# Feature-major copies of a graph network's inputs: TensorE transposes exchanged for VectorE blocks and trips through DRAM

## The chip, the cores and the metric

One core of one Trainium2 chip. The metric is the device time of one execution in microseconds; each kernel was run several times and the median is quoted. A ratio is the mean time of one kernel's fast runs over that of the other's of the same rounds, so it is not quite the ratio of the medians quoted beside it.

## The reference

64 graphs of 256 nodes with 128 features pass through four layers that share one adjacency matrix; each layer ends in `layernorm(x + layer(x))`.

```python
def reference(x, adj, ...):                        # x (64, 256, 128), all float32
    x = layernorm(x + pair_attention(x, adj, ...))          # layer 0
    x = layernorm(x + graph_attention(x, adj, ...))         # layer 1
    x = layernorm(x + gated(x, adj, ...))                   # layer 2, five steps of:
    #   m = adj @ h; u = h @ U3; z = sigmoid(m @ W3 + u); r = sigmoid(m @ W4 + u)
    #   h = (1 - z) * h + z * tanh(m @ W5 + (r * h) @ U5)
    x = layernorm(x + chebyshev(x, adj, ...))               # layer 3: x, adj@x, adj@adj@x, ...
    return x
```

The kernel's products over features read x with features on the partitions ("feature-major"); its products with the adjacency read it with nodes there ("token-major"). Turning one into the other is what the change is about.

## The kernel before

A unit is two graphs, a tile of 128 by 512 floats. There are 32 units and seven lanes, so seven units are in flight. The order of instructions on every engine is fixed at build time by a small list scheduler, the planner, with booked durations and latencies. TensorE transposes each layer's input:

```python
    def feature_major(u, L, name="xT0"):            # layers 0, 2 and 3 call it
        ps = bank()
        for g in range(G):                           # G = 4
            add(PE, 110, lambda g=g: nc.tensor.transpose(
                ps.ap[:, g * P : (g + 1) * P], X[u].ap[:, g // NC, g % NC, :], ident.ap), (X[u], ident), (ps,))
        add(ACT, 500, lambda: nc.scalar.copy(L[name].ap, ps.ap), (ps,), (L[name],))
        return L[name]
```

Inside the gated layer the way back to token-major already went through DRAM for most units: VectorE turns 32 by 32 blocks (705 ns for a tile in the profile of this kernel), one store puts them in a DRAM tile, four loads collect them in another order. I call this a trip.

```python
            if step < STEPS - 1 and u < NU - NEAR:   # NEAR = 3, NU = 32
                add(DVE, 600, lambda h=h, v=v: nc.vector.transpose(...), (h,), (v,))
                add("sp", 450, lambda v=v: nc.sync.dma_start(L["hb"].ap, v.ap), (v,), (L["hb"],))
                for a in range(D // BL):             # four loads
                    add("sp", 450, lambda a=a: nc.sync.dma_start(...), (L["hb"],), (ht,), wait=1000)
                continue
```

How the planner books this:

```python
    LATENCY = {"pe": 700, "dve": 600, "act": 600, "pool": 700, "sp": 5000}
    OWN = {"pe": 0, "dve": 70, "act": 70, "pool": 100, "sp": 0}
    # end of a task = start + its ns + LATENCY of its engine + its wait
    def seen_at(self, t, by):                        # when `by` may start after `t`
        return t.end if t.eng != by.eng else t.off + self.OWN[t.eng]
```

All transfers are issued by one engine, "sp" (SyncE's queue).

The softmax here doesn't subtract the row's maximum and nothing guards it: scores larger than these inputs give would overflow.

## Time and profile before

| | before |
|---|---|
| median | 1518.3 us |
| span of the profiled run | 1511.7 us |
| TensorE busy / rest of the span | 1470.5 / 41.2 us |
| TensorE's waits for trips | 11.2 us in 10 waits |
| granted TensorE clock | 0.997 |

TensorE is the bound: busy 97% of the span.

### The profile page before, as it was taken

What the parts mean: (1) busy time and instruction counts of PE and PEld (TensorE: products, weight loads), DVE (VectorE), ACT (ScalarE), POOL (GpSimd) and SP (SyncE); (2) the same over time, 40 slices, a digit from 0 to 9 for tenths busy, and PEclk for the clock granted to TensorE, in tenths of its full rate; (3) what the DMA queues carried; (4) which work ended last, traced back from release to release, by engine and by line L of the source; (5) the groups of instructions that cost most, each with busy time, mean ns of one, the idle gap of its engine ahead of it and who ended that gap; (6) DMA issues with size and microseconds to landing.
All of it is one profiled execution on the core that took longest, in us unless ns stands there. A gap on an engine that the chain in (4) does not pass through costs nothing.

```text
span 1511.7 us, 18346 instructions
## 1 busy us (share of the span) xinstructions
PE 1470.5 (97%) x6081; PEld 993.9 (66%) x6081; DVE 1028.4 (68%) x2485; ACT 762.8 (50%) x1455; POOL 148.8 (10%) x134
## 2 busy tenths in 40 slices
PE   8899998999999999999999999999999999999998
PEld 7565575666567576666666675766666666665566
DVE  6975648876666776767667777677577767664554
ACT  4664435655545554456454555456355554554432
POOL 0200011110001011010010110101001001000011
PEclk9999999999999999999999999999999999999999
DMA  5123323223232323232332233232332322220001
GB/s 151 27 67 76 77 49 73 57 61 79 56 87 55 75 65 84 50 81 70 74 73 60 65 71 85 47 76 66 71 67 53 75 59 62 58 56 15 15 8 42
DMA packets 323952, 95.93 MB, mean 63 GB/s; under 512 B 267409, under 2 KB 301457, under 8 KB 323857
## 3 DMA queue, kind: packets, MB, share of 16 engines
q1 hardware_dynamic: 323856, 94.76, 27.6%
q8 instruction: 48, 0.79, 0.2%
q14 instruction: 48, 0.39, 0.1%
HBM read 55.67 MB, written 39.03 MB: 63 GB/s over the span
## 4 chain that ended last, share of the span: by engine, by line
PE 87%; DMA 5%; DVE 4%; SPq 2%; ACT 1%; issue 0%; POOLq 0%; DVEq 0%
PE ps L635 42%; PE ps L615 20%; PE ps L703 7%; PE ps L710 4%; PE ps L547 3%; PE ps L577 3%; PE ps L413 2%; PE ps L481 2%; PE ps L591 2%; PE ps L542 1%; DMA ht<-hb 1%; SPq L670 1%; DMA hb<-p 1%; PE ps L677 1%; DVE st L446 0%
## 5 line engine op out<-in xcount | busy, mean ns | idle before, releaser
L635 PE MATMUL ps<-m,gT 128*128 128x512 f32 x960 | 464.3, 593 | 1.3 <-ACT m L631 0.9
L451 POOL TENSOR_TENSOR rstd<-ve,nhalf 128x4 f32<-128x4 f32 x128 | 148.1, 1159 | 1357.6 <-DVE ve L448 1303.8
L635 PEld LDWEIGHTS ps<-m,gT 128*128 128x128 f32 x960 | 175.7, 190 | 139.7 <-issue 119.3
L615 PE MATMUL ps<-adjTp,ht 128*128 128x256 f32 x928 | 234.2, 380 | 11.8 <-DMA ht<-hb 11.2
L615 PEld LDWEIGHTS ps<-adjTp,ht 128*128 128x128 f32 x928 | 172.4, 190 | 90.9 <-issue 64.4
L654 DVE TENSOR_TENSOR p<-p,xT 128x512 f32<-128x512 f32 x160 | 109.8, 687 | 130.8 <-ACT p L648 130.5
L650 ACT ACTIVATE e<-ps,bias 128x512 f32<-128x512 f32 x160 | 109.8, 686 | 131.6 <-PE ps L635 131.2
L641 ACT ACTIVATE e<-ps,bias 128x512 f32<-128x512 f32 x160 | 109.7, 686 | 125.5 <-PE ps L635 125.2
L631 ACT COPY m<-ps 128x512 f32<-128x512 f32 x160 | 93.5, 584 | 151.8 <-PE ps L615 151.6
L635 PE MATMUL ps<-xT,gT 128*128 128x512 f32 x320 | 162.2, 593 | 2.4 <-ACT xT L415 1.3
L635 PE MATMUL ps<-e,u5T 128*128 128x512 f32 x320 | 162.5, 593 | 1.6 <-DVE e L643 1.6
L643 DVE SCALAR_TENSOR_TENSOR e<-e,xT 128x512 f32<-128x512 f32 x160 | 109.2, 684 | 77.7 <-ACT e L641 77.7
L648 ACT ACTIVATE p<-ps,bias 128x512 f32<-128x512 f32 x160 | 109.9, 687 | 82.0 <-PE ps L635 76.8
L615 PE MATMUL ps<-adjT,x 128*128 128x256 f32 x512 | 142.1, 380 | 0.0
L655 DVE SCALAR_TENSOR_TENSOR p<-e,p 128x512 f32<-128x512 f32 x160 | 109.3, 684 | 21.0 <-ACT e L650 18.6
L657 DVE SCALAR_TENSOR_TENSOR xT<-p,xT 128x512 f32<-128x512 f32 x160 | 109.6, 686 | 2.4
L615 PEld LDWEIGHTS ps<-adjT,x 128*128 128x128 f32 x512 | 84.3, 191 | 38.5 <-issue 25.7
L446 DVE BATCH_NORM_STATS2 st<-ps 128x6 f32<-128x256 f32 x128 | 53.3, 425 | 70.1 <-PE ps L710 51.2
L415 ACT COPY xT<-ps 128x512 f32<-128x512 f32 x96 | 55.9, 584 | 72.4 <-PE ps L413 72.0
L635 PEld LDWEIGHTS ps<-e,u5T 128*128 128x128 f32 x320 | 58.7, 190 | 48.2 <-issue 35.2
L566 ACT ACTIVATE e<-m,esd 128x256 f32<-128x256 f32 x116 | 84.3, 760 | 8.1 <-DMA m<-row 8.1
L413 PE MATMUL ps<-ident,x 128*128 128x128 f32 x384 | 82.4, 277 | 2.6 <-DMA x<-in_x_dram 2.5
(131 smaller groups left out, 1954.5 us busy)
## 6 DMA issues: line engine op xcount, KB each, us to landing
hb<-p SPq DMA_DIRECT2D x116, 256.0 KB, 2.1
ht<-hb SPq DMA_DIRECT2D x464, 64.0 KB, 2.5
m<-row SPq DMA_DIRECT2D x58, 256.0 KB, 3.6
x<-in_x_dram SPq DMA_DIRECT2D x32, 256.0 KB, 3.3
out_dram<-x SPq DMA_DIRECT2D x32, 256.0 KB, 2.4
u<-rowu SPq DMA_DIRECT2D x58, 3.8 KB, 3.1
row<-cu SPq DMA_DIRECT2D x29, 2.0 KB, 2.1
rowu<-cu SPq DMA_DIRECT2D x29, 4.0 KB, 1.7
```

Source lines behind the costliest of these rows:

```text
L413: add(PE, 110, lambda g=g: nc.tensor.transpose(ps.ap[:, g * P : (g + 1) * P], X[u].ap[:, g // NC, g % NC, :], ident.ap), (X[u], ident), (ps,))
L451: add(POOL, 1050, lambda: nc.gpsimd.tensor_tensor(rstd.ap, ve.ap, nhalf.ap, op=ALU.pow), (ve, nhalf), (rstd,))
L615: add(PE, mm_ns(N), lambda b=b, mc=mc: nc.tensor.matmul(ps.ap[:, b * N : (b + 1) * N], lhs(b, mc), mat.ap[:, mc, :], start=(mc == 0), stop ...
L635: add(PE, mm_ns(T), lambda: nc.tensor.matmul(ps.ap, w(), rhs.ap, start=start, stop=stop, skip_group_check=True), (c, rhs), (ps,))
L641: add(ACT, 600, lambda ps_g=ps_g: nc.scalar.activation(r.ap, ps_g.ap, AF.Tanh, bias=bias2.ap[:, 1:2], scale=0.5), (ps_g, bias2), (r,))
L643: add(DVE, 600, lambda h=h: nc.vector.scalar_tensor_tensor(r.ap, r.ap, 1.0, h.ap, op0=ALU.add, op1=ALU.mult), (r, h), (r,))
L648: add(ACT, 600, lambda ps_v=ps_v: nc.scalar.activation(v.ap, ps_v.ap, AF.Tanh, bias=bias2.ap[:, 2:3]), (ps_v, bias2), (v,))
L650: add(ACT, 600, lambda ps_g=ps_g: nc.scalar.activation(z.ap, ps_g.ap, AF.Tanh, bias=bias2.ap[:, 0:1], scale=0.5), (ps_g, bias2), (z,))
L654: add(DVE, 600, lambda h=h: nc.vector.tensor_sub(v.ap, v.ap, h.ap), (v, h), (v,))
L655: add(DVE, 600, lambda: nc.vector.scalar_tensor_tensor(v.ap, z.ap, 1.0, v.ap, op0=ALU.add, op1=ALU.mult), (v, z), (v,))
L657: add(DVE, 600, lambda h=h, new=new: nc.vector.scalar_tensor_tensor(new.ap, v.ap, 0.5, h.ap, op0=ALU.mult, op1=ALU.add), (v, h), (new,))
L703: add(PE, mm_ns(N), lambda k=k, src=src, c=c, b=b: nc.tensor.matmul(view(c)[:, :, b, :], bn(src.ap)[:, b, c * P : (c + 1) * P], w3.ap[:, k ...
```

## The change

The intent is to take transposes off the bounding engine. Layer 0's x is loaded in four blocks of 32 features, so that one VectorE transpose of 32 by 32 blocks finishes it (701 ns in the profile after; the first seven units still use TensorE). The inputs of layers 2 and 3 of units 3 to 30 are turned by VectorE and a trip. The border of the gated layer's own trips moves to the same units. Also, the load of the x that a lane needs next moves from before layer 0 to after it, and x gets separate tiles (`zs`) to land in.

```diff
-NEAR = 3
+NEAR = 1
 ...
     def load_x(u):
+        z = zs[u % LANES]
+        if u < LANES:
+            add("sp", 1000, lambda: nc.sync.dma_start(z.ap..., x_u[u]), (), (z,))
+            return
+        for a in range(D // BL):
+            add("sp", 450, lambda a=a: nc.sync.dma_start(z.ap[a * BL : (a + 1) * BL]..., x_a[u, a]...), (), (z,), wait=1000)
 ...
+    def far(u):
+        return DIRECT <= u < NU - NEAR               # DIRECT = 3
+    def turned(u, L, name="xT0"):                     # layers 2 and 3
+        t = L[name]
+        if not far(u):
+            feature_major(X[u], ..., t)
+            return t
+        v = L["v"]
+        add(DVE, 1050, lambda: nc.vector.transpose(
+            v.ap.rearrange("p (a g i) -> p g a i", g=G, i=BL),
+            X[u].ap.rearrange("p b c (j a) -> p (b c) a j", j=BL)), (X[u],), (v,))
+        add("sp", 450, lambda: nc.sync.dma_start(L["hb"].ap, v.ap), (v,), (L["hb"],))
+        for q in range(P // BL):
+            add("sp", 450, lambda q=q: nc.sync.dma_start(t.ap...[:, :, q], L["hb"].ap[...]...), (L["hb"],), (t,), wait=1000)
+        return t
 ...
     def layer0(u, L):
-        xT = feature_major(u, L)
+        xT, z = L["xT0"], zs[u % LANES]
+        if u < LANES:
+            feature_major(z, ..., xT)
+        else:
+            add(DVE, 600, lambda: nc.vector.transpose(xT.ap, z.ap), (z,), (xT,))
 ...
-            if step < STEPS - 1 and u < NU - NEAR:
+            if step < STEPS - 1 and far(u):
```

More of the change, by code (lines that the diff above doesn't have):

```diff
@@ L223 @@
     x_u = x.rearrange("(u b) (c p) d -> u p b c d", b=UB, p=P)
+    x_a = x.rearrange("(u b) n (a i) -> u a (b n) i", b=UB, i=BL)
     out_u = out.rearrange("(u b) (c p) d -> u p b c d", b=UB, p=P)
-    xs, X = [cell(f"x{k}", [P, UB, NC, D]) for k in range(2 * LANES)], {}
+    zs = [cell(f"z{k}", [P, T]) for k in range(LANES)]
     def load_x(u):
-        X[u] = c = xs[u % len(xs)]
-        add("sp", 1000, lambda: nc.sync.dma_start(c.ap, x_u[u]), (), (c,))
+        z = zs[u % LANES]
+        if u < LANES:
+            add("sp", 1000, lambda: nc.sync.dma_start(z.ap.rearrange("p (b c d) -> p b c d", b=UB, c=NC), x_u[u]), (), (z,))
+            return
+        for a in range(D // BL):
+            add("sp", 450, lambda a=a: nc.sync.dma_start(
+                z.ap[a * BL : (a + 1) * BL].rearrange("j (b i) -> j b i", i=BL),
+                x_a[u, a].rearrange("(b j) i -> j b i", j=BL)), (), (z,), wait=1000)
     w1 = load("w1", W, [D, D])
@@ L387, in lane_cells @@
             c[name] = Cell(c[at].ap.rearrange("p g n -> p (g n)")[:, half * T : (half + 1) * T])
+        c["x"] = cell(f"x_{k}", [P, UB, NC, D])
         c["h0"] = cell(f"h0_{k}", [P, G, C0])
@@ L399, in lane_cells @@
         return c
+    X = {}
     lanes = [lane_cells(k) for k in range(LANES)]
@@ L407, in bn, with feature_major @@
         return ap.rearrange("p (b n) -> p b n", b=UB)
-    def feature_major(u, L, name="xT0"):
+    def far(u):
+        return DIRECT <= u < NU - NEAR
+    def feature_major(src, view, t):
         ps = bank()
         for g in range(G):
-            add(PE, 110, lambda g=g: nc.tensor.transpose(
-                ps.ap[:, g * P : (g + 1) * P], X[u].ap[:, g // NC, g % NC, :], ident.ap), (X[u], ident), (ps,))
-        add(ACT, 500, lambda: nc.scalar.copy(L[name].ap, ps.ap), (ps,), (L[name],))
-        return L[name]
+            add(PE, 110, lambda g=g: nc.tensor.transpose(ps.ap[:, g * P : (g + 1) * P], view(g), ident.ap),
+                (src, ident), (ps,))
+        add(ACT, 500, lambda: nc.scalar.copy(t.ap, ps.ap), (ps,), (t,))
+    def turned(u, L, name="xT0"):
+        t = L[name]
+        if not far(u):
+            feature_major(X[u], lambda g: X[u].ap[:, g // NC, g % NC, :], t)
+            return t
[5 more added lines that the diff above has]
+        for q in range(P // BL):
+            add("sp", 450, lambda q=q: nc.sync.dma_start(
+                t.ap.rearrange("p (g q i) -> p g q i", g=G, i=BL)[:, :, q],
+                L["hb"].ap[q * BL : (q + 1) * BL].rearrange("j (a g i) -> (j a) g i", g=G, i=BL)),
+                (L["hb"],), (t,), wait=1000)
+        return t
     def to_row(row, src, view, n):
@@ L469, in layer0 @@
     def layer0(u, L):
-        xT = feature_major(u, L)
+        xT, z = L["xT0"], zs[u % LANES]
+        if u < LANES:
+            feature_major(z, lambda g: gd(z.ap)[:, g], xT)
+        else:
+            add(DVE, 600, lambda: nc.vector.transpose(xT.ap, z.ap), (z,), (xT,))
+        X[u] = L["x"]
         xb = bn(xT.ap)
@@ L619, in layer2 @@
     def layer2(u, L):
-        h, ht = feature_major(u, L), X[u]
+        h, ht = turned(u, L), X[u]
         for step in range(STEPS):
@@ L625, in layer2 @@
                     left(ps_m, ht, b)
-                elif u < NU - NEAR:
+                elif far(u):
                     left(ps_m, ht, b, lambda b, mc: gd(ht.ap)[:, b * NC + mc], adjTp)
@@ L687, in layer3 @@
     def layer3(u, L):
-        xT = feature_major(u, L)
+        xT = turned(u, L)
         ps_a, aT, s = bank(), L["m"], L["z"]
@@ L716, in spawn @@
     def spawn(u, lane):
-        if u + LANES < NU:
-            load_x(u + LANES)
         for k, layer in enumerate((layer0, layer1, layer2, layer3)):
@@ L721, in spawn @@
             layer(u, lanes[lane])
+            if not k and u + LANES < NU:
+                load_x(u + LANES)
     def first(t):
```

## The prediction

> **What bounds the kernel now.** I read the page's busy shares first, then TensorE's waits, then a stretch of TensorE's timeline to get the price of one transpose, then the queue of DMA issues, because the change takes work from TensorE and gives it to that queue. Busy shares (engine, busy us, share of the span, instructions):
>
> ```profile
> span 1511.7 us, 18346 instructions
> ...
> PE 1470.5 (97%) x6081; PEld 993.9 (66%) x6081; DVE 1028.4 (68%) x2485; ACT 762.8 (50%) x1455; POOL 148.8 (10%) x134
> ...
> PE 87%; DMA 5%; DVE 4%; SPq 2%; ACT 1%; issue 0%; POOLq 0%; DVEq 0%
> ```
>
> The last line is the chain that ended last: 87% of it is TensorE. No other engine is near its limit. In the table of windows TensorE idles some 25 us before 350 us, 10 us from there to 950, none from 950 to 1490, and 7 us at the end. Who it waited for (total us, times, longest):
>
> ```profile
> PE ps L615 <- DMA ht<-hb: 11.2, 10, 1.9
> PE ps L317 <- DMA w<-in_L_gnn_W_dram: 2.8, 1, 2.8
> PE ps L577 <- DVE p L570: 2.7, 1, 2.7
> PE ps L413 <- DMA x<-in_x_dram: 2.5, 3, 1.5
> ```
>
> The only repeated wait is for a tile that came back through DRAM (ht from hb). It is small, but it is the wait that this change multiplies. So the first-order rule is: a microsecond of TensorE stream removed is a microsecond of span, unless the replacement arrives late.
>
> **Price of a transpose.** The groups by line give 277 ns as the mean of one, but that is the duration of a pipelined record, not what it takes from the stream. The timeline of TensorE (start, us, instruction, count) shows the real price:
>
> ```profile
> 303.25 1.02 PE L635 MATMUL ps<-m,gT 128*128 128x512 f32 x2
> 304.11 0.59 PE L615 MATMUL ps<-adjTp,ht 128*128 128x256 f32 x2
> 304.55 0.60 PE L413 MATMUL ps<-ident,x 128*128 128x128 f32 x4
> 304.98 0.60 PE L615 MATMUL ps<-adjTp,ht 128*128 128x256 f32 x2
> ```
>
> Four transposes of layer input (L413) start at 304.55 and the next product starts at 304.98: 0.43 us for four, 0.108 us each. Where single ones stand between matmuls (1426.48 to 1426.59) it is 0.11 us as well.
>
> [...]
> - [...] 277 ns of duration against 108 ns of spacing. Hence I price by spacing.
> - [...] each group of four is followed by a 584 ns ScalarE copy, so both go together.
> - [...] The new VectorE transpose before the trip through DRAM reads with a stride of four floats[...]. The only VectorE transpose in this trace (L665, 705 ns) reads without that stride[...]; I take 1.1 to 1.2 us as my estimate, by the ratio of L511, which reads its m with a stride at 607 ns for 256 columns, to L515 at 343 ns.
> [...]
>
> **The change part by part.** I counted the instructions of both builds in program order.
> 1. TensorE. Layer 0: 25 of 32 units lose their four transposes (the first seven keep them): -100. Layers 2 and 3: 28 units, 3 to 30, lose four each: -224. The border of the gated layer's DRAM path moves from units 0-28 to 3-30: units 0 to 2 now make 4 steps of 4 transposes on TensorE, units 29 and 30 no longer: +48 - 32 = +16. Sum -308. At 0.108 us: **33.3 us off the stream**, 2.2% of 1518.6.
> 2. ScalarE: 81 copies fewer, 4 more: 77 x 584 ns = 45 us off an engine that is half idle. Worth nothing directly; it frees PSUM banks earlier.
> 3. VectorE: 25 plain transposes x 0.7, 56 strided ones x about 1.15, four of the old kind fewer: 17.5 + 64 - 3 = +79 us, so 1107 us in about 1490, 74% against 68%. Still below TensorE, but its waiting lines grow a little.
> 4. DMA engines: a trip through DRAM is 2048 packets of 128 bytes on the way back plus 128 rows on the way out; 52 trips more net, and 25 x loads go from 512-byte rows to 128-byte pieces (+1536 each). About +151,000 packets on 324,000; the queue's 27.6% share becomes some 40%. Not a bound.
> 5. The DMA queue on SyncE. This is the disputed cost. One trip and the next look like this (start, us of issuing):
>
> ```profile
> 630.34 0.33 SPq L668 DMA_DIRECT2D hb<-p  x1
> 632.39 2.54 SPq L670 DMA_DIRECT2D ht<-hb  x4
> 635.10 0.50 SPq L668 DMA_DIRECT2D hb<-p  x1
> 637.35 2.54 SPq L670 DMA_DIRECT2D ht<-hb  x4
> ```
>
> The queue is in order: it issues the store (0.33), stands until that has landed (about 2), then issues four loads (2.5): 4.9 us per trip. Its own waits, whole run:
>
> ```profile
> SPq L670 <- DMA hb<-p: 226.3, 115, 3.9
> SPq L668 <- DVE p L665: 193.0, 44, 19.3
> SPq L714 <- DVE x L460: 131.4, 15, 55.9
> SPq L668 <- DVE x L460: 96.0, 15, 21.1
> ```
>
> From 550 to 950 us the same list sums to 104 us of standing for DMA landings and 152 us of standing for engines; the remaining 144 us are issuing. So the queue is truly occupied 62%, and 38% is waiting for work. The change adds, per unit of 47 us, two trips (9.8 us) and four block loads at 0.62 us for one of 0.47 (2.0 us): 11.8 us, 25 points. The queue goes to roughly **87%**. It stays under TensorE's load, so it does not become the bound by sum, but a queue that full delays its customers.
>
> How much delay can be taken? I paired each returned ht of the trace with the first matmul that reads it: half wait at least 3.9 us after landing, a quarter 2.3 us or less, a tenth 0.2 us or less. Today a store's issue lags its VectorE transpose by 1.5 us in the median and 3.7 us at the ninth decile. With the queue at 87% I expect lags a few microseconds longer, and 168 trips to suffer them instead of 116. The new xT trips have some shelter: in both layers 2 and 3 the adjacency product of the same unit reads X directly and goes first. A stall of TensorE also lets the queue catch up, so stalls do not simply add. I estimate TensorE's DMA waits to rise from 11 us to about 20 to 25: **+9 to +14 us**. The end: units 29 and 30 now take trips while few others are left; TensorE was full there until 1490, so I add **0 to 2 us**. Head: the first seven units load as before; 0.
>
> Sum: 1518.6 - 33.3 + about 12 to 15 puts the middle at 1497 to 1500; the choice of units looks tuned against just these waits, which is a reason to lean to the lower side, and I settle on **1495 us**.
>
> **Rivals.**
> - *Everything hides.* For it: from 950 to 1400 us no TensorE wait at all was seen although trips went on; seven units are in flight; the plan books 5 us for each landing where about 2 to 2.5 are measured. Against: a quarter of the present returns have little slack. Then 1518.6 - 33.3 gives 1485, perhaps 1480 with freer PSUM banks.
> - *The queue takes the place of TensorE.* For it: 87%, in order, a store that blocks everything behind it, and a plan that books 0.45 us per issue where 0.62 is measured. Against: 38% idle today is mostly real slack. Then DMA waits grow to 40 or more and the time is 1505 to 1520.
> - *VectorE's added 79 us lengthens every chain.* For it: each gated step has five VectorE operations in series. Against: 74% is moderate and TensorE waits for VectorE only a few microseconds now. By itself worth under 5 us: 1490 in the hidden case.
>
> **Range and chances.** The lower end, 1480, is full hiding with a little extra; the upper, 1513, is the queue rival at half strength or more. Faster by over 2% means under 1488.2, that is at most 3 us of the 33 given back. I give that 0.33. Slower by over 2% needs some 64 us of new stalls; 0.02. The rest, 0.65, lies within.
>
> **What would show it.** TensorE's list of waits: ht from hb and the new xT from hb together at 20 to 25 us; under 14 speaks for hiding, over 40 for the queue. SyncE's own waits for engines should shrink to near a third of today's. TensorE's instruction count should fall by 308 and its busy time by about the stream's 33 us or somewhat more. The strided transpose should show 1.1 to 1.2 us; at 0.7 VectorE's part was oversized, at 2 it was undersized. I am wrong if the span falls by under 10 us without larger DMA waits (then the transposes did not cost stream time), or if the gain is over 40 us.

Its sum reads 1518.6 - 33.3 + 12 to 15 us, 1497 to 1500, settled at 1495. The 1.1 to 1.2 us of the strided transpose is the estimate from L511 and L515; it enters VectorE's load, not the sum.

## More of the kernel before

The experiments ran in other sessions than the first comparison; in each of them the kernel before was timed again (1513.9 us in the first two, 1519.0 in the third), so compare ratios across sessions, not bare times. The record lists three different chips for them (7, 5 and 9).

## The result, and the profile after

The changed kernel takes **1614.5 us** (median of four) against 1518.3: ratio 1.0626, 95% interval 1.0593 to 1.0658. It is 96 us slower, where 33 us of TensorE work were removed. Its busy shares and its chain that ended last:

```profile
span 1611.7 us, 18392 instructions
...
PE 1479.9 (92%) x5773; PEld 984.5 (61%) x5773; DVE 1094.2 (68%) x2562; ACT 724.0 (45%) x1378; POOL 150.9 (9%) x134
...
PE 63%; DMA 16%; DVE 12%; SPq 6%; ACT 2%; issue 2%; DVEq 0%; ACTq 0%
```

Two things to see. TensorE has 308 instructions fewer and is nevertheless busy 9 us longer. And the rest of the span, in which it stands idle, went from 41 to 132 us. In the chain TensorE fell from 87% to 63%; DMA and the DMA queue ("SPq") rose from 7% to 22%, and VectorE ("DVE") from 4% to 12%; an experiment below leaves VectorE's new work in and shows that it isn't the cause. TensorE's longest waits by sum:

```profile
PE ps L654 <- DMA ht<-hb: 45.6, 20, 7.2
PE ps L742 <- DMA xT<-hb: 18.3, 6, 5.2
PE ps L674 <- DVE e L682: 9.5, 5, 3.6
PE ps L674 <- DMA xT<-hb: 5.8, 6, 2.4
```

The old trips (ht) cost most: four times what they did, although there are four fewer of them. The new trips (xT) cost 24 us. TensorE's other waits, mostly for VectorE and ScalarE, rose too, from 23 to 55 us; that these follow from the late tiles is not shown one by one. So whatever happened, it happened also to transfers that the change hardly touched.

The busy time is explained by a table of windows (start to end, length, then busy us and count of each engine, granted TensorE clock, DMA share, GB/s). Before:

```profile
550.00:650.00 100.00, 99.77 (x407) 66.86 (x406) 65.75 (x158) 50.88 (x97) 8.36 (x7) 1.00 0.30 69
1050.00:1150.00 100.00, 100.00 (x410) 68.17 (x409) 70.58 (x169) 50.09 (x96) 11.91 (x10) 1.00 0.28 64
```

After:

```profile
550.00:650.00 100.00, 89.70 (x318) 57.64 (x317) 69.63 (x161) 46.88 (x86) 9.84 (x8) 0.93 0.37 82
1050.00:1150.00 100.00, 82.30 (x329) 55.38 (x327) 62.52 (x156) 43.53 (x89) 10.91 (x8) 0.91 0.33 74
```

In the two windows after, where TensorE idles 10 and 18 us, the clock it is granted (third number from the right) is lower too, 0.93 and 0.91. The trace's clock records resolve this: between 60 us and the last 15 us the kernel before has no stretch under full clock; the changed one has 19, each 3.4 or 6.8 us long at half clock, 78 us together. At half clock those lose 39 us. Of the 20 idle gaps of TensorE of over 2.3 us here, 17 have such a stretch beginning within 3 us of their end; the kernel before has no such gap after its start. That is an association in the trace; no run varied the gaps alone.

So the span's 100 us can be put together from three numbers: -33 us (308 transposes at 0.108), +91 us of idle, +39 us of half clock, 97 in all. (Of the 39, 5 us fall into idle gaps and are counted twice.)

One stall at close range, 7.25 us at 1129 us, shows how the idle arises. The queue's own timeline (start, us of issuing, what):

```profile
1116.21 0.56 SPq L707 DMA_DIRECT2D hb<-p  x1
1120.52 4.56 SPq L709 DMA_DIRECT2D ht<-hb  x7
1125.17 0.56 SPq L444 DMA_DIRECT2D hb<-p  x1
1127.65 1.19 SPq L446 DMA_DIRECT2D xT<-hb  x2
1128.94 0.57 SPq L707 DMA_DIRECT2D hb<-p  x1
1131.51 2.73 SPq L709 DMA_DIRECT2D ht<-hb  x4
```

and TensorE's:

```profile
1127.18 1.97 PE L654 MATMUL ps<-adjTp,ht 128*128 128x256 f32 x8 [0.30 <-DMA ht<-hb]
1136.40 1.19 PE L654 MATMUL ps<-adjTp,ht 128*128 128x256 f32 x2 [7.25 <-DMA ht<-hb]
```

Pairing the store at 1128.94 with its VectorE transpose in program order, I find that this was finished at 1118.66. The blocks then lay there for 10.3 us, because the queue stood until an earlier store had landed (issued at 1116.21, landed at 1120.45: 4.2 us, against a median of 2.5), issued seven loads, then issued another store, stood again (1125.17 to 1127.6), and issued two loads. But for that one landing nothing was slow; the tile stood in line.

Over all trips, from the end of the VectorE transpose to the landing of the last load: median 7.4 us before, 10.2 us after; ninth decile 11.4 and 17.1. The planner allows at least 8.85 us for this (0.6 after VectorE, 0.45 for the store, 1.8 for the loads, 6.0 for the landing; an expectation below leaves the 0.6 out and says 8.25), and puts TensorE's reader of the tile in its order accordingly. Before, 38 of 116 trips took longer than that; after, 109 of 168.

### The profile page after: what moved, and what is told of

Same layout as the page of the kernel before. It is cut to its first block, busy times and chain, and to the rows that moved or that the text cites. A ratio compares the mean times of both kernels' runs of the same rounds, so it can differ in the third digit from the quotient of the medians.

```text
span 1611.7 us, 18392 instructions
## 1 busy us (share of the span) xinstructions
PE 1479.9 (92%) x5773; PEld 984.5 (61%) x5773; DVE 1094.2 (68%) x2562; ACT 724.0 (45%) x1378; POOL 150.9 (9%) x134
## 2 busy tenths in 40 slices
DMA packets 480864, 123.21 MB, mean 76 GB/s; under 512 B 430464, under 2 KB 451712, under 8 KB 480768
## 4 chain that ended last, share of the span: by engine, by line
PE 63%; DMA 16%; DVE 12%; SPq 6%; ACT 2%; issue 2%; DVEq 0%; ACTq 0%
PE ps L674 29%; PE ps L654 14%; PE ps L742 6%; DMA hb<-p 4%; PE ps L749 3%; SPq L709 3%; DMA xT<-hb 2%; PE ps L586 2%; PE ps L616 2%; DMA ht<-hb 2%; DMA u<-rowu 2%; DMA row<-cu 2%; PE ps L520 1%; PE ps L581 1%; SPq L446 1%
## 5 line engine op out<-in xcount | busy, mean ns | idle before, releaser
L674 PE MATMUL ps<-m,gT 128*128 128x512 f32 x960 | 469.9, 601 | 8.8 <-ACT e L680 5.7
L654 PE MATMUL ps<-adjTp,ht 128*128 128x256 f32 x896 | 239.9, 400 | 55.7 <-DMA ht<-hb 45.6
L674 PEld LDWEIGHTS ps<-m,gT 128*128 128x128 f32 x960 | 180.7, 194 | 156.8 <-issue 129.1
L654 PEld LDWEIGHTS ps<-adjTp,ht 128*128 128x128 f32 x896 | 174.3, 200 | 142.0 <-issue 89.8
L674 PE MATMUL ps<-xT,gT 128*128 128x512 f32 x320 | 166.6, 607 | 11.6 <-DMA xT<-hb 5.8
L654 PE MATMUL ps<-adjT,x 128*128 128x256 f32 x512 | 132.5, 381 | 0.0
L654 PEld LDWEIGHTS ps<-adjT,x 128*128 128x128 f32 x512 | 95.4, 192 | 43.7 <-issue 32.2
L674 PEld LDWEIGHTS ps<-xT,gT 128*128 128x128 f32 x320 | 59.3, 194 | 56.2 <-issue 33.7
L742 PE MATMUL ps<-w,xT 128*128 128x256 f32 x256 | 69.2, 404 | 18.9 <-DMA xT<-hb 18.3
```

The source lines that it names most:

```text
L654: add(PE, mm_ns(N), lambda b=b, mc=mc: nc.tensor.matmul(ps.ap[:, b * N : (b + 1) * N], lhs(b, mc), mat.ap[:, mc, :], start=(mc == 0), stop ...
L674: add(PE, mm_ns(T), lambda: nc.tensor.matmul(ps.ap, w(), rhs.ap, start=start, stop=stop, skip_group_check=True), (c, rhs), (ps,))
L742: add(PE, mm_ns(N), lambda k=k, src=src, c=c, b=b: nc.tensor.matmul(view(c)[:, :, b, :], bn(src.ap)[:, b, c * P : (c + 1) * P], w3.ap[:, k ...
```

## The experiments

Theory: the trips clog SyncE's in-order queue; tiles come back later than the planner assumed; TensorE, whose order is fixed as well, stands; and half clock is recorded around the end of most of its long stands (17 of the 20 above). Rivals: the blocks of x; VectorE's added work; DMA engines or DRAM overloaded; the latency of the new trips in their own unit's chain.

**One part alone: the blocks of x.**

```diff
-NEAR = 1
+NEAR = 3
     def far(u):
-        return DIRECT <= u < NU - NEAR
+        return u < NU - NEAR
 ...
-        if not far(u):                # in turned(): always TensorE
+        if True:
```

> Only layer 0's x in feature-major blocks; layers 2 and 3 transposed on TensorE and the gated layer's border as before. 100 transposes fewer than before, worth 10.8 us of stream; four block loads of 0.62 us per unit in place of one of 0.5 on the DMA queue. If the trips through DRAM are what costs (theory: the in-order DMA queue is delayed by the trips), this is harmless: 1505 to 1515 us, clock 0.99. If the blocks or the later load of x are to blame, 1540 us or more and TensorE waits for z.

Measured: 1517.4 us, ratio 1.0022 (1.0005 to 1.0039). The blocks are not what costs 96 us. But it was a miss: the 10.8 us did not show. Idle rose by 10 us and half clock took 7; waits for ht were unchanged (11.5 us), so other waits of the new order did this, together some 17 us. Which ones I did not settle.

**One part alone: the trips.**

```diff
     def load_x(u):
-        if u < LANES:
+        if True:                      # rows for all units
 ...
     def layer0(u, L):
-        if u < LANES:
+        if True:                      # TensorE for all units
```

> Only the trips through DRAM of layers 2 and 3 (units 3 to 30); layer 0 loads x in rows and transposes on TensorE for all units. Theory (trips delay the queue): nearly all of the loss stays, 1580 to 1620 us, clock 0.97 to 0.98, waits for ht and xT together 40 us or more. If the blocks of x were the cause, 1495 to 1520.

Measured: 1578.9 us, ratio 1.0432, clock 0.981, waits for ht and xT 54 us. Two thirds of the loss; a little under the range. The rest comes with the blocks, which put four loads per unit on the same queue. In idle and half clock together (the ledger below) trips alone cost 82 us, blocks alone 17, and both 130: more than the sum.

**The trip left out (wrong result).** VectorE writes its blocks straight into xT:

```diff
-        v = L["v"]
-        add(DVE, 1050, lambda: nc.vector.transpose(v.ap..., X[u].ap...), (X[u],), (v,))
-        add("sp", 450, ...store...)
-        for q in range(P // BL): add("sp", 450, ...load...)
+        add(DVE, 1050, lambda: nc.vector.transpose(t.ap..., X[u].ap...), (X[u],), (t,))
```

> The changed kernel with the VectorE transpose kept and the trip through DRAM of layers 2 and 3 left out: the transposed blocks go straight to xT, so the result is wrong on purpose. Shows what the removed transposes are worth when no new DMA wait is put in. If my 0.108 us a transpose is right and VectorE's added work is free: 1480 to 1490 us, clock 0.99. If VectorE's added 79 us is what lengthens the chains: 1530 us or more.

Measured: 1484.0 us, ratio 0.9803, clock 0.994. The transposes were worth 30 us, near the 33 predicted, and VectorE's added work, which is still there, costs little: 3 us lie between the two numbers. That rival falls.

**Trips that nobody reads, in the kernel before.** At the same two places of units 3 to 30:

```diff
+    def dummy_trip(u, L):
+        add("sp", 450, lambda: nc.sync.dma_start(L["hd"].ap, X[u].ap...), (X[u],), (L["hd"],))
+        for q in range(P // BL):
+            add("sp", 450, lambda q=q: nc.sync.dma_start(L["dm"].ap..., L["hd"].ap[...]...), (L["hd"],), (L["dm"],), wait=1000)
```

> The kernel before, with 56 extra trips through DRAM (store and four loads as in the change, at the same two places of units 3 to 30) whose result nobody reads. TensorE keeps all its transposes and waits for none of these trips. Theory (the queue is in order, and what stands behind a trip comes late): the old ht trips come late, 1550 to 1610 us, clock under 0.99, waits for ht 30 us or more. Rival (the loss is TensorE waiting for the new trips themselves, their latency in the unit's own chain): 1515 to 1530 us.

Measured: 1606.2 us, ratio 1.0614, clock 0.972. Its first wait:

```profile
PE ps L627 <- DMA ht<-hb: 43.9, 19, 7.8
```

TensorE never waits for a dummy. The new trips' own latency is therefore not needed for the loss: 56 bystanders on the queue produce 92 us, the same clock and the same late ht (76 of 116 old trips past 8.85 us). These 92 us are not to be set against the net 96: nothing was saved here, while the changed kernel lost some 130 us and had 33 of it covered by the transposes. By the ledger below the bystanders lost 98, three quarters of that.

**The same dummies without standing.** The loads read the input x in place of what the store wrote:

```diff
-                L["hd"].ap[q * BL : (q + 1) * BL]..., (L["hd"],), (L["dm"],), wait=1000)
+                x_h[u][q * BL : (q + 1) * BL]...,     (),         (L["dm"],), wait=1000)
```

> The kernel before with the same 56 dummy stores and 224 dummy loads as the run that cost 92 us, but the loads read the input x in DRAM and not what the store wrote: same sizes, same 128-byte pieces, same issue time, and the queue no longer stands about 2 us per trip for the store's landing. If it is the standing that delays the rest: half or more of the 92 us goes, 1530 to 1560 us. If it is the traffic on the DMA engines or the time of issuing: 1585 us or more.

Measured: 1560.9 us, ratio 1.0315, just past the expected end: 45 of the 92 us go. I meant this to isolate the standing, but it doesn't. Running the planner of this kernel alone shows that, with no store to wait for, it puts all 224 loads ahead of their store in the queue, so the order changed too. That half of the loss is the standing is not shown.

**The same dummies from ScalarE's queue.** The planner books 0.62 us per load and 2.1 us between a store and its loads for these alone:

```diff
-        add("sp", 450, lambda: nc.sync.dma_start(...), ...)
+        add(ACT, 450, lambda: nc.scalar.dma_start(...), ..., dma=True)
-            add("sp", 450, lambda q=q: nc.sync.dma_start(...), ...)
+            add(ACT, 620, lambda q=q: nc.scalar.dma_start(...), ..., dma=True)
```

> The kernel before with the same dummy trips, store and dependent loads, issued from ScalarE's queue and not SyncE's. The DMA engines carry the same packets. If SyncE's in-order queue is the cause: 1515 to 1545 us (ScalarE pays some 3 us of issuing per trip, 170 us on an engine that is half idle), waits for ht near 11 us. If DMA engines or DRAM are overloaded: 1580 us or more, and landing times stay long.

Measured: 1540.7 us, ratio 1.0181; waits for ht 18.7 us, where near 11 was expected. The same bytes cost 27 us there in place of 92. So at least 65 of the 92 us are SyncE's queue and the order around it, not the DMA engines. Queue and booking are not told apart here, since these dummies were also booked right. What the remaining 27 are, ScalarE's own standing or traffic, stays open.

**Same instructions, other booking.** The changed kernel with the planner told what the queue really does:

```diff
-    LATENCY = {..., "sp": 5000}
+    LATENCY = {..., "sp": 3000}
     def seen_at(self, t, by):
+        if t.eng == by.eng == "sp" and t in by.raw:   # by reads what t wrote
+            return t.off + 2100
 ...
-            add("sp", 450, ...each 64 KB load of blocks or of a trip...)
+            add("sp", 620, ...)
```

> The changed kernel, same instructions, other order: the planner books 620 ns for each 64 KB load in place of 450, lets a load that reads a store issue only 2.1 us after it, so that other transfers slide in between, and adds 3 us in place of 5 for a landing, so that a trip is booked at about 9 us in all against 8.25. Theory (the loss is the order made for a queue that the plan thought 40% full, so that TensorE stands in order for late tiles): 1490 to 1530 us, TensorE's DMA waits under 35 us, clock 0.985 or more. If the queue simply has too much to do whatever the order: 1580 us or more.

Measured: **1472.3 us**, ratio 0.9727 (0.9711 to 0.9743), better than expected: faster than both kernels, with a correct result. The work is the same; only the order changed. TensorE's waits for trips fell from 70 us in 32 waits to 3.4 us in 3, where under 35 us was expected:

```profile
PE ps L678 <- DMA xT<-hb: 1.7, 1, 1.7
PE ps L746 <- DMA xT<-hb: 1.2, 1, 1.2
...
PE ps L658 <- DMA ht<-hb: 0.5, 1, 0.5
```

Lines of its page:

```profile
span 1470.8 us, 18372 instructions
...
PE 1437.3 (98%) x5773; PEld 970.2 (66%) x5773; DVE 1097.6 (75%) x2562; ACT 724.2 (49%) x1378; POOL 148.1 (10%) x134
...
DMA packets 480864, 123.21 MB, mean 84 GB/s; under 512 B 430464, under 2 KB 451712, under 8 KB 480768
```

The packets are those of the slow order, moved faster (84 against 76 GB/s): the DMA engines were never the limit. TensorE's busy time is 33 us under before's 1470.5, which is the price of 308 transposes. The queue, where a stand used to be:

```profile
1013.54 0.38 SPq L711 DMA_DIRECT2D hb<-p  x1
1014.55 0.33 SPq L448 DMA_DIRECT2D hb<-p  x1
1015.73 2.56 SPq L713 DMA_DIRECT2D ht<-hb  x4
1018.45 1.19 SPq L450 DMA_DIRECT2D xT<-hb  x2
1019.69 0.62 SPq L711 DMA_DIRECT2D hb<-p  x1
```

Two stores are issued before the first one's loads; the second lands while those are issued (its own loads follow them at 1018.45). From 550 to 950 us the queue's 400 us divide as follows (its list of waits summed; issuing is the remainder):

| | issuing | standing for landings | waiting for engines |
|---|---|---|---|
| before | 144 | 104 | 152 |
| after | 186 | 130 | 85 |
| after, booked | 209 | 40 | 152 |

More transfers per microsecond, and yet as much slack as before. Over the whole run the queue of the changed kernel stood 352 us for the landing of trips' stores, in 165 waits.

**Control: the same booking in the kernel before.**

> Control: the same booking in the kernel before. Its queue is 62% occupied and its waits are 11 us, so there is little to win: 1500 to 1520 us. If it gains as many microseconds as the changed kernel does, the booking is a general gain and not the cure of this change's loss.

Measured: 1495.2 us, ratio 0.9881. A little under the expected range. It gains 19 us; the changed kernel gains 136 (0.0899 between its two ratios, times 1516). So most of the cure belongs to this change's loss, and a small part is general. The idle outside TensorE's busy time falls from 41 to 24 us: part of what looked like unavoidable idle was this too.

**The booking with the blocks of x alone.**

> Layer 0's blocks alone with the new booking; layers 2 and 3 transposed on TensorE. Against the changed kernel with the same booking (1472 us) it has 208 transposes more, 22.5 us of stream at 0.108. If trips through DRAM are harmless once the queue is booked right: 1490 to 1500 us. If they still cost what they save: 1472 or less.

Measured: 1484.8 us, ratio 0.9779, below the expected range and between its two branches. Next to 0.9727 the 208 further transposes are worth 0.5%, some 8 us (5 to 11 by the two intervals), and not 22: the trips still give back half or more of what they save.

**The two halves of the booking, each on the changed kernel.** First only the shorter landing (`"sp": 3000`):

> The changed kernel with only one half of the booking: 3 us in place of 5 for a landing, and the queue's own time booked as before. If the cure was the right account of the queue's time, this alone takes slack away and makes it worse than the changed kernel: 1620 us or more. If the cure was that the plan no longer holds tiles back for a landing that takes 2.5 us: 1500 us or less.

Measured: 1648.8 us, ratio 1.0862, clock 0.960: worse, as a planner that allows less time for the same late tiles must be.

Then only the account of the queue's time (620 ns and 2.1 us, landing as before):

> The other half: 620 ns per load and 2.1 us between a store and the loads that read it, landing still booked at 5 us. If the account of the queue's time is the cure: most of the 142 us comes back, 1480 to 1540 us, some of it lost because a trip is then booked at about 11 us and tiles are held back longer than they need be. If both halves are needed: 1570 us or more.

Measured: 1495.1 us, ratio 0.9850. This half alone turns 6% slower into 1.5% faster. The shorter landing is worth having only after it. The 620 ns and the 2.1 us were not tried one by one, nor was the new order of the queue tried apart from the new order of TensorE, so which of these does most stays open.

**Booked against measured.** The planner is plain Python, so each kernel's order can be booked again without the chip and every trip's own booking set beside its measured time:

| run | planned end, us | measured span, us | trips later than their own booking |
|---|---|---|---|
| before | 1511 | 1512 | 31 of 116 |
| after | 1479 | 1612 | 107 of 168 |
| after, short landing | 1461 | 1642 | 135 of 168 |
| after, queue's time booked | 1525 | 1492 | 0 of 168 |
| after, booked | 1488 | 1471 | 8 of 168 |
| before, booked | 1509 | 1493 | 4 of 116 |

The plan that promised the shortest time gave the longest.

**The ledger.** For each profiled run but the first: transposes removed at 0.108 us; change of the span outside TensorE's busy time; half of the time at half clock after the start; their sum; and the change of the span against 1511.7.

| run | transposes | idle | half clock | sum | span |
|---|---|---|---|---|---|
| after | -33 | +91 | +39 | +97 | +100 |
| blocks only | -11 | +10 | +7 | +6 | +5 |
| trips only | -22 | +56 | +26 | +60 | +64 |
| no trip | -33 | 0 | +2 | -32 | -29 |
| dummies | 0 | +59 | +39 | +98 | +98 |
| dummies without standing | 0 | +32 | +14 | +46 | +46 |
| dummies, ScalarE | 0 | +17 | +12 | +28 | +28 |
| after, short landing | -33 | +106 | +58 | +131 | +131 |
| after, queue's time booked | -33 | +8 | +7 | -19 | -20 |
| after, booked | -33 | -8 | +2 | -39 | -41 |
| before, booked | 0 | -17 | 0 | -17 | -19 |
| blocks, booked | -11 | -13 | 0 | -24 | -29 |

The terms are rounded after summing. They close to within 5 us in every row; without the half clock that falls into idle gaps (at most 10 us, in the short landing), to within 10. Since span is busy time plus idle, what this tests is that TensorE's busy time changed by the transposes and the half clock and by little else.

## Why the prediction was wrong

The measured time lies where the prediction gave a chance of 0.02.

- *Price of the transposes, 33 us:* right. Leaving out the trip gave 30, and the booked run's busy time fell by 33.
- *ScalarE, VectorE, DMA engines:* right, or nearly. ScalarE lost 39 us of work (predicted 45). The strided VectorE transpose took 1101 ns (predicted 1.1 to 1.2 us; the plain one 705), which was in part luck: the ratio behind it, 607 to 343 ns, set an operation on two tiles (L511) against one on a tile and a scalar (L515), and these kinds differ without any stride too, 687 to 422 ns at 512 columns (L654, L599). VectorE was busy 1094 us (predicted 1107); 480,864 packets (predicted 475,000); the DMA engines' share 35% (predicted 40).
- *Queue occupied 87%:* measured 79% in that stretch of the slower run. As a load it was well estimated; it could have been carried, as the booked order shows with all of it in 62%. SyncE's waits for engines fell from 152 to 85 us in that stretch, not to near a third.
- *Delay turned into time, "+9 to +14 us":* **this step failed.** Idle cost 91 us. It rested on three statements that do not hold. "The plan books 5 us for each landing" is not so for a load behind a store on the same queue: `OWN["sp"]` is 0, so the stand of about 2 us is booked as nothing and the whole trip as 8.85 us. I had the code before me and took the latency from one line without the exception two lines on. "A stall also lets the queue catch up, so stalls do not simply add" was an argument without a number; 32 waits on trips added to 70 us, past the 40 that the prediction itself had named as the sign of the queue. And the lag that I gave as 1.5 us in the median and 3.7 at the ninth decile was misread by one column: the median is 0.03 us, 1.5 is the upper quartile. It became 2.0, 5.1 and 8.5 (median, upper quartile, ninth decile), "a few microseconds longer" as said, but the margin in the plan was just over one (8.85 booked against a median of 7.4).
- *Shelter of the xT trips:* wrong. Readers of xT waited 24 us in 12 waits.
- *The clock:* absent from the prediction. Longest trip wait before 1.9 us, no half clock between 60 us and the end's last 15; after, waits up to 7.2 us and 39 us lost on top.
- *The end, 0 to 2 us:* right; TensorE is full from 1450 to 1590 us.
- *Rivals:* "the queue takes the place of TensorE" had the mechanism and the evidence, but its 1505 to 1520 us was undersized by 95; the range ended at 1513.

## What to carry to other kernels

Before moving work off the bounding engine onto an in-order queue, compare what the scheduler books for each transfer with what the trace shows, standing included: here a fixed order made for a queue thought emptier than it is cost 130 us of TensorE's time once most tiles (107 of 168) came later than booked. A cheap test beforehand is to add the new transfers to the old kernel with no reader; here that cost 92 us, which already outweighed the 33 us to be saved.
